# A graph layer's kernel: seven products of quarters for two product pairs in matrices 8 and 9 too

## The chip, the cores and the metric

The kernel runs on one core of one Trainium2 chip. Its time is the device time of one execution in microseconds (us); the time before is the median of three runs, 1374.24 us (1372.67 to 1378.07). A core has engines that run side by side, each through a queue of its own in order: TensorE (PE) multiplies, VectorE (DVE) and ScalarE (ACT) add, scale and copy, GpSimd (POOL) here mainly issues gathers and scatters by index, and SyncE (SP) issues plain transfers. ScalarE issues some transfers too. They meet through semaphores.

## The reference

One relational graph layer over 1250 nodes of 1024 features, 20000 edges and 8 edge types, with a highway gate; all in 32-bit floats:

```
h = max(layernorm(x), 0)
u = h @ root + bias
for r in 0..7:
    sums = segment_sum(h[src] where edge type is r, dst); cnt = count of such edges per dst
    u += (sums / max(cnt, 1)) @ weight[r]
z = concat(u, h) @ w_gate + b_gate
out = x + tanh(u) * z + h * (1 - z)
```

## The kernel before

Averaging over edges and multiplying by a weight can change places, so the kernel first multiplies h by every matrix and then gathers rows of the products by edge. The matrices are numbered s = 0 to 10: eight relation weights (0 to 7), root (8, `ROOT`), the lower half of w_gate, which multiplies h (9), and the upper half, which multiplies u (10). `NM` is 11, `R0` is (0, 3, 6, 8): the relations form three groups. Products of relations go to `y` in HBM, that of root to `hr_dram`, that of matrix 9 to `z_dram`; the last two get a bias added in `put` (L499), from the tile `bias_bc`.

**Steps.** The 1250 rows are ten blocks of up to 128 rows. `step(s, i)` multiplies two of them, blocks i and i + 5, by matrix s; `NP` = 5 steps make a matrix. Each is a 256x1024 by 1024x1024 product, done by the Strassen-Winograd scheme on halves: seven products (A11 B11, A12 B21, S1 T1, S2 T2, S3 T3, S4 B22, A22 T4) in `product`, each four matmuls of 128x512 (L377, which the trace records as two passes each). S1 to S4 are sums of quarters of h, kept in `h_op`; T1 to T4 are sums of quarters of the matrix, kept in nine buffers `wbuf` and made by VectorE (`make_t1` to `make_t4`, L169 to L181) around the end of the matrix before. Matrix 8's root and 9's and 10's weights are loaded from the last two steps of the matrix before on, by ScalarE's and SP's queues.

**Products of two neighbouring steps.** Two neighbouring steps use the same right operand, so their two 128-row products of one kind form a 256x512 by 512x512 product, and this can be done by the same scheme once more, on quarters: seven products of two 128x256 matmuls each (L214) in place of two of four 128x512 matmuls. Three classes do so:

- `Second`, for A12 B21 of steps 0 and 1, and of steps 2 and 3, in all matrices from 1 on.
- `Third`, for S4 B22 of the same two pairs, where `thirds(s)` holds: matrices 4 to 7.
- `Fourth`, for A22 T4 of steps 1 and 2, and of steps 3 and 4, in the same matrices.

`Third` and `Fourth` need sums of their quarters, made by VectorE just in time: `sums` (L270 to L273: s1, t1, s2, t2), and later `next_sums` (L276 to L279), which write the next values over them. They stand in the four tiles `room`, from a pool `inner` that is open while matrices 4 to 7 run. `first` makes three quarter products and has ScalarE copy two of them into a `part` tile (L294, L297); `last` makes three more, and `second` the seventh. VectorE adds them to the rows in `first_to` (L305, L306), `fifth_to` (L309) and `last_to` (L312 to L314, L329 to L333).

**Rows.** The results of a step are two row tiles of 128x1024 out of four `row` buffers. `put` stores a row with SP's queue when all of its parts have been added. With `Third` the first row of an even step is put in the step after it (from `then`), and with `Fourth` the second row of an odd step is put at the end of the step after it.

**Gathers.** Beside the products run the edges' sums, one group of relations beside two matrices: group 0 beside 4 and 5, group 1 beside 6 and 7, group 2 (`LG`) beside 8 and 9. For each block of nodes VectorE multiplies each gathered row by its weight and adds it to `u` (`add_slot`, L1218); GpSimd issues the gathers (L1210) into four `got` buffers. There are four `u` buffers. Beside 8 and 9 the blocks are taken in the order 4 to 9, 0 to 3, with 4, 4, 3, 3, 2, 2, 16, 7, 6 and 5 slots; a block's u is loaded by GpSimd (`rows_of`, L630), and the first six are stored by SP (`last_dram`, L1422) when done. Between matrices 7 and 8 stands a conditional branch for nodes with unusually many edges (L1353); it isn't taken in the traced execution.

The program is scheduled by hand: on each engine the instructions stand in the order in which the Python code issues them. `beside(j)` in `step` is called after each product of a step with j counting up, and decides what VectorE and the transfer queues get between products; gathers are spread evenly over these calls, at its end (`between`).

Of the kernel before, what the change touches and what calls it, by code (L numbers as in the profile page):

```python
# [9 lines left out]
F32 = mybir.dt.float32  # L10
# [9 lines left out]
def tile_rgcn_highway(  # L20
# [31 lines left out]
    nc = tc.nc  # L52
# [3 lines left out]
    P = 128  # L56
    N, D = x.shape
# [5 lines left out]
    H = Q // 2  # L63
# [4 lines left out]
    G = 3  # L68
    R0 = (0, 3, 6, R)
# [20 lines left out]
    def nrows(d):  # L90
        return min(P, N - d * P)
# [4 lines left out]
    def nedges(c):  # L96
        return P if c < NCH - 1 else EL
# [366 lines left out]
    ROOT = R  # L464
# [8 lines left out]

    def thirds(s):

        return R0[1] < s < ROOT

    def fourths(s, i):

        return (i - 1) // 2 * 2 + 1 if thirds(s) and i else None  # L480
# [3 lines left out]
    def step(s, i, between=lambda j: None, second=None):  # L484

        two = paired(s, i)
        t = [rows.tile([P, D], F32, name="row") for _ in range(2)]
# [5 lines left out]
        def put(i, part, t):  # L493
            d = i + part * NP
            n = nrows(d)
            at = slice(d * P, d * P + n)
            if s >= ROOT:
                to = (hr_dram, z_dram)[s - ROOT][at, :]
                nc.vector.tensor_add(t, t, bias_bc)  # L499
            else:  # L500
                g = max(k for k in range(G) if R0[k] <= s)
                o = (s - R0[g]) * N + d * P
                to = y[g][o:o + n, :]
            nc.sync.dma_start(to, t[:n])

        def beside(j):
# [17 lines left out]
            if q4 and i % 2 == 0 and j == 6:  # L524
                q4.last_to(to4, t[1][:, :Q])
                put(i - 1, 1, t4)
# [38 lines left out]
        if two:  # L565
            e, to = waiting[i - i % 2]
            if thirds(s):
                if i % 2 == 0:
                    waiting_third[i] = Third(fac[s], i, room)
                q = waiting_third[i - i % 2]  # L570
                q.holds = i % 2 == 0

                def then(c):
                    if q.holds:
                        q.second(c)
                    else:
                        q.last(c)
                        q.last_to(to[:, Q:], t[0][:, Q:], c)
                        put(i - 1, 0, to)

                q.then = then
            if i == 0:
                fill = dict(sixth=lambda: (e.second(), e.second_to_first(to)))
            elif i == 1:
                fill = dict(first=lambda: (e.first(), q and q.first(), 0)[-1],
                            fifth=lambda: (e.sixth(), True),
                            sixth=lambda: (e.seventh(), e.to_first(to), 0)[-1],
                            seventh=lambda: (e.fourth(), e.to_second(t[0]),
                                             q or put(i - 1, 0, to), 0)[-1],
                            third=lambda: (e.fourth_to_second(t[0]), 0)[-1])  # L590
            elif i == 2:
                fill = dict(sixth=lambda: (e.first(), q4 and q4.first(), q4)[-1],
                            seventh=lambda: e.sixth(),
                            third=lambda: (e.seventh(), e.to_first(to), 0)[-1],
                            fourth=lambda: (e.fourth(), not q4)[-1])
            else:
                fill = dict(first=lambda: (e.to_second(t[0]), e.fourth_to_second(t[0]), 0)[-1],
                            sixth=lambda: (e.second(), q and q.first(), True)[-1],
                            seventh=lambda: (e.second_to_first(to), q or put(i - 1, 0, to),
                                             0)[-1])  # L600
# [17 lines left out]
    idx = const.tile([P, G, ND, WIDE], I32, name="idx")  # L618
    rcp = idx.bitcast(F32)[:, :, :, SLOTS:]
    w_of = const.tile([P, G, ND, SLOTS], F32, name="w_of")  # L620
# [65 lines left out]
    with ExitStack() as early:  # L686
# [108 lines left out]
        for name, of, pad in (("dst", dst, G * KEYS), ("typ", etype, R), ("src", src, 0)):  # L795
            t = ix0.tile([P, 2, P], I32, name=f"e_{name}")
# [374 lines left out]
        while going[0]:  # L1171
            s, i = next(steps)
# [11 lines left out]
    with ExitStack() as edges_part:  # L1184
# [6 lines left out]
        room = [inner_pool.tile([P, 2, n], F32, name=f"inner{k}")  # L1191
                for k, n in enumerate((H, H, P, P))]
# [37 lines left out]
        def edges(g, blocks, to, late=0):  # L1230

            of = u_dram[g - 1] if g else None
            nb = len(blocks)
            starts = [late + sum(K[g][d] for d in blocks[:b]) for b in range(nb + 1)]
            leaves = [starts[b + 1] - 1 + GOT for b in range(nb)]
            reads = [max(-1, starts[b] - 5, leaves[b - UB] if b >= UB else -1) for b in range(nb)]
            u, then = {}, {}  # L1240
            for t in range(-1, leaves[-1] + 4):
                for b, d in enumerate(blocks):
                    if starts[b] <= t < starts[b + 1]:
                        k = t - starts[b]
                        add_slot(u[d], g, d, k, idx[:, g], w_of[:, g], first=g == 0 and k == 0)
                for b, d in enumerate(blocks):
                    if t == leaves[b]:
                        then[t + 3] = to(d, u[d])
                if then.get(t):
                    then[t]()  # L1250
                for b, d in enumerate(blocks):
                    if t == reads[b]:
                        u[d] = new_u(d, of, g)
                yield

        def u_back(g):
            def to(d, u):
                n = nrows(d)
                to_rows(u_dram[g][:, :], u[:n], node[:n, g, d:d + 1], f"u{g}")

            return to
# [42 lines left out]
        def beside(e, total, s, i, last):  # L1304


            between = spread(e, total, 7 * ((last - s) * NP + NP - i))
            while s <= last:
                step(s, i, between)
                s, i = next(steps, (NM, 0))  # L1310
            return s, i

        s, i = next(steps)
        while s <= R0[1]:
            step(s, i)
            s, i = next(steps)
# [8 lines left out]
        def with_others(e):  # L1325

            others = other_groups()
            for k, _ in enumerate(e):
                yield
                if k % 2:  # L1330
                    next(others, None)
            for _ in others:
                pass

        weights(0)
        s, i = beside(with_others(edges(0, range(ND), u_back(0))), sum(K[0]) + 2, s, i,
                      R0[2] - 1)
# [6 lines left out]
        for g in range(1, G - 1):  # L1344
# [3 lines left out]
            s, i = beside(e, sum(K[g]) + LATE + 1, s, i, R0[g + 2] - 1)  # L1348
# [4 lines left out]
        with tc.If(passes > 0):  # L1353
# [34 lines left out]
            with tc.For_i(0, passes, 1):  # L1388
# [9 lines left out]
                for c in range(NCH):  # L1398
                    n = nedges(c)
# [11 lines left out]


        inner_part.close()
        bias_bc = edges_part.enter_context(tc.tile_pool(name="bpool", bufs=1)).tile(
            [P, D], F32, name="bias_bc")
        nc.sync.dma_start(bias_bc, bias[None, :].to_broadcast([P, D]))
        LG = G - 1
        HELD = 4

# [59 lines left out]
        def gate_u(i, j):  # L1479

            if j == 2:
                for part, d, n in pair(i):
                    hs[part] = got()
                    rows_of(hs[part][:n], h_dram[:, :], node[:n, LG, d:d + 1])
                    nc.scalar.activation(place_of("d", i, part)[:n], us[d][:n], AF.Tanh)
            elif j == 3:
                for part, d, n in pair(i):
                    transposed(h_op[i % 2], part, us.pop(d), n)
                left(h_op[i % 2])
            elif j == 4:  # L1490
                for part, d, n in pair(i):
                    dt = place_of("d", i, part)
                    nc.vector.tensor_sub(dt[:n], dt[:n], hs[part][:n])
# [16 lines left out]
        while s < NM - 1:  # L1510
            def beside_h(j):
                between(j)
                if (s, i, j) == (ROOT + 1, 0, 0):
                    nc.sync.dma_start(bias_bc, b_gate[None, :].to_broadcast([P, D]))
                if (s, i) == (NM - 2, NP - 1):
                    gate_u(0, j)

            step(s, i, beside_h)
            s, i = next(steps, (NM, 0))

        for i in range(NP):
            t = [rows.tile([P, D], F32, name="row") for _ in range(2)]
# [54 lines left out]
            else:  # L1577
# [3 lines left out]
                                                                  bufs=2)))  # L1581
# [22 lines left out]
```

## Time and profile before

The profile is of one execution. Its engines' busy times by matrix are shown with the prediction; here is the frame.

| | |
|---|---|
| time of the profiled execution | 1378.07 us |
| its span (first to last instruction) | 1376.3 us |
| median of three runs | 1374.24 us |
| instructions | 13466 |
| granted TensorE clock, mean | 0.993 |
| start of matrices 4, 5, 6, 7 | 515.85, 636.57, 767.05, 882.63 |
| start of matrices 8, 9, 10 | 1003.41, 1122.17, 1240.93 |
| VectorE busy in matrices 8 and 9 | 68.48 and 76.18 us |
| matmul rows of 128x512 (L377), 128x256 (L214) | 2480 in `ps`; 288 and 248 in the two largest groups |

Times inside an execution are us from the span's start. A timeline line gives start, duration, engine, source line, operation, out<-in, and in brackets the idle time of the engine before it with what ended it. A matmul's shown duration overlaps the next one's, so the distance between starts is the true cost. "q" after an engine's name is its sequencer: it issues a transfer. A wait that is put down to an engine is the one that ended last.

### The profile page before, as it was taken

What the parts mean: (1) busy time and instruction counts of PE and PEld (TensorE: products, weight loads), DVE (VectorE), ACT (ScalarE), POOL (GpSimd) and SP (SyncE); (2) the same over time, 40 slices, a digit from 0 to 9 for tenths busy, and PEclk for the clock granted to TensorE, in tenths of its full rate; (3) what the DMA queues carried; (4) which work ended last, traced back from release to release, by engine and by line L of the source; (5) the groups of instructions that cost most, each with busy time, mean ns of one, the idle gap of its engine ahead of it and who ended that gap; (6) DMA issues with size and microseconds to landing.
All of it is one profiled execution on the core that took longest, in us unless ns stands there. A gap on an engine that the chain in (4) does not pass through costs nothing.

```text
span 1376.3 us, 13466 instructions
## 1 busy us (share of the span) xinstructions
PE 1343.0 (98%) x4002; PEld 698.1 (51%) x4002; DVE 1023.6 (74%) x2049; ACT 376.7 (27%) x824; POOL 653.7 (47%) x571
## 2 busy tenths in 40 slices
PE   9999999999999999998899999999999999999998
PEld 5444455455445545654465566556455445544443
DVE  7855967887884976877688778978765485567985
ACT  3335566565641111110111121111111111121220
POOL 0001655564562468647665344566534244435641
PEclk9999999999999999999899999999999999999999
DMA  8745566754763257288878647878866664586861
GB/s 318 265 181 144 94 127 150 197 92 109 174 164 112 57 163 171 70 298 168 257 229 319 201 141 259 300 254 296 318 208 241 219 251 137 179 300 216 279 222 58
DMA packets 110654, 273.06 MB, mean 198 GB/s; under 512 B 26020, under 2 KB 28434, under 8 KB 110448
## 3 DMA queue, kind: packets, MB, share of 16 engines
q0 software_dynamic: 48912, 128.60, 30.3%
q1 hardware_dynamic: 45536, 111.58, 27.2%
q10 hardware_dynamic: 16128, 31.98, 7.2%
q8 instruction: 32, 0.52, 0.2%
q14 instruction: 46, 0.38, 0.1%
HBM read 214.20 MB, written 80.89 MB: 214 GB/s over the span
## 4 chain that ended last, share of the span: by engine, by line
PE 57%; issue 15%; DMA 11%; DVE 9%; POOL 6%; ACT 1%; POOLq 0%; DVEq 0%; another core or an unknown queue 0%; ACTq 0%
PE ps L377 47%; DMA got<-y,idx 8%; PE ps L214 6%; DVE u L1218 2%; POOL got L1210 2%; DMA y<-row 2%; PE ps_q L214 1%; POOL node_dram L667 1%; POOL idx L630 1%; PE ps_n L377 1%; DMA node_dram<-ids,pos_i 1%; POOL got L630 1%; PE ps_n L947 1%; DMA got<-hr_dram,node 1%; POOL out_dram L636 1%
## 5 line engine op out<-in xcount | busy, mean ns | idle before, releaser
L377 PE MATMUL ps<-w,h_op 128*128 128x512 f32 x2480 | 1092.0, 594 | 15.6 <-ACT row L427 13.4
L377 PEld LDWEIGHTS ps<-w,h_op 128*128 128x128 f32 x2480 | 466.8, 190 | 551.8 <-issue 526.4
L1210 POOL DMA_INDIRECT got<-y,idx x202 | 266.5, 1319 | 241.3 <-DVE u L1218 173.6
L1218 DVE SCALAR_TENSOR_TENSOR u<-got,w_of,u 128x1024 f32<-128x1024 f32 (+1 forms) x192 | 245.9, 1282 | 113.7 <-DMA got<-y,idx 104.1
L1026 POOL DMA_INDIRECT table<-row_col,at_i x157 | 177.0, 1127 | 163.5 <-DVE at_i L1022 73.8
L402 DVE TENSOR_TENSOR row<-row,part 128x512 f32<-128x512 f32 x55 | 37.9, 689 | 70.6 <-ACT part L401 61.8
L453 ACT COPY row<-ps 128x512 f32<-128x512 f32 x50 | 29.2, 584 | 200.5 <-PE ps L377 127.2
L401 ACT COPY part<-ps 128x512 f32<-128x512 f32 x55 | 32.2, 585 | 174.7 <-PE ps L377 162.3
L416 ACT COPY row<-ps 128x512 f32<-128x512 f32 x55 | 32.2, 585 | 164.8 <-PE ps L377 144.5
L214 PE MATMUL ps<-w,w 128*128 128x256 f32 x288 | 71.3, 380 | 0.0
L427 ACT COPY row<-ps 128x512 f32<-128x512 f32 x55 | 32.2, 585 | 129.0 <-PE ps L377 120.7
L423 ACT COPY row<-ps 128x512 f32<-128x512 f32 x47 | 27.5, 585 | 138.8 <-PE ps L377 102.4
L667 POOL DMA_INDIRECT node_dram<-ids,pos_i x30 | 43.7, 1457 | 44.6 <-issue 44.3
L214 PE MATMUL ps<-w,h_op 128*128 128x256 f32 x248 | 64.2, 381 | 0.0
L214 PEld LDWEIGHTS ps<-w,w 128*128 128x128 f32 x288 | 54.4, 190 | 19.2 <-issue 13.2
L214 PEld LDWEIGHTS ps<-w,h_op 128*128 128x128 f32 x248 | 46.6, 190 | 24.7 <-issue 20.7
L952 DVE TENSOR_TENSOR seen<-seen,ps_n 128x110 f32<-128x110 f32 x157 | 42.2, 269 | 21.7 <-PE ps_n L947 10.0
L1012 DVE SCALAR_TENSOR_TENSOR junk<-k_bc,key_col,before 128x128 f32<-128x128 int32 x157 | 54.9, 350 | 4.2
L394 DVE TENSOR_TENSOR row<-row,ps 128x512 f32<-128x512 f32 x38 | 26.0, 685 | 42.2 <-PE ps L377 28.7
L929 ACT ACTIVATE is_lo<-io,less_lo 128x128 bf16<-128x128 f32 x157 | 50.1, 391 | 0.7 <-DMA xh_dram<-xt 0.7
L1080 DVE SCALAR_TENSOR_TENSOR junk<-v_bc,val,one 128x1280 bf16<-128x1280 f32 x30 | 46.5, 1550 | 0.8
L630 POOL DMA_INDIRECT u<-u_dram,node x20 | 20.4, 1020 | 51.3 <-DMA last_dram<-u 32.0
(223 smaller groups left out, 1328.5 us busy)
## 6 DMA issues: line engine op xcount, KB each, us to landing
y<-row SPq DMA_DIRECT2D x72, 512.0 KB
w<-in_L_gnn_weight_dram ACTq DMA_DIRECT2D x21, 1024.0 KB
w<-in_L_gnn_weight_dram SPq DMA_DIRECT2D x10, 1024.0 KB
k_bc<-keys_dram SPq DMA_DIRECT2D x39, 256.0 KB
l_bc<-los_dram SPq DMA_DIRECT2D x39, 256.0 KB
w<-in_L_gnn_w_gate_dram ACTq DMA_DIRECT2D x6, 1024.0 KB
h_dram<-h_op SPq DMA_DIRECT2D x9, 512.0 KB
hr_dram<-row SPq DMA_DIRECT2D x9, 512.0 KB
```

Of the source, the lines that this page charges most:

```text
L214: nc.tensor.matmul(p, a[:, k, :], b[:, k, :], start=(fresh and k == 0), stop=(k == 1), skip_group_check=True)
L377: nc.tensor.matmul(b[:, at], aop[:, i, k, :], w.of[i][:, k, at], start=(fresh and k == 0), stop=(k == KQ - 1), skip_group_check=True)
L402: nc.vector.tensor_add(c22, c22, d)
L630: nc.gpsimd.indirect_dma_start(out=to, out_offset=None, in_=of, in_offset=bass.IndirectOffsetOnAxis(ap=at, axis=0))
L667: ins = nc.gpsimd.indirect_dma_start(out=node_dram[g][:, :], out_offset=bass.IndirectOffsetOnAxis(ap=pos_i[:, g, d:d + 1], axis=0), in_=id ...
L929: nc.scalar.activation(is_lo[:, i, :], io, AF.Abs, bias=less_lo[:, c0 + i:c0 + i + 1])
L952: nc.vector.tensor_add(seen[j][:, i, :], was, p[:, i, :])
L1012: nc.vector.scalar_tensor_tensor(junk, o["k_bc"][:, i, :], key_col[:, c:c + 1], before, op0=OP.is_equal, op1=OP.mult, accum_out=rank[:, c: ...
L1026: ins = nc.gpsimd.indirect_dma_start(out=table[:, :], out_offset=bass.IndirectOffsetOnAxis(ap=at_i[:n, i:i + 1], axis=0), in_=row_col[:n, ...
L1080: nc.vector.scalar_tensor_tensor(junk, v_bc[:, g, :], val[:, c:c + 1], one.to_broadcast([P, KEYS]), op0=OP.is_gt, op1=OP.mult, accum_out=p ...
L1210: nc.gpsimd.indirect_dma_start(out=t[:n], out_offset=None, in_=y[g][:, :], in_offset=bass.IndirectOffsetOnAxis(ap=at[:n, d, k:k + 1], axis=0),
L1218: nc.vector.scalar_tensor_tensor(u[:n], t[:n], w, u[:n], op0=OP.mult, op1=OP.add)
```

## The change

`thirds` holds for every matrix after 3 up to 9 (matrix 10 is not made by `step`), so `Third` and `Fourth` are used in matrices 8 and 9. Their sums need a place when the pool `inner` has been closed: the two of 128x512 get tiles of a new pool, and the two of 128x256 are put over the part of the index tile `idx` that groups 0 and 1 no longer need. To make room, `bias_bc` becomes two pieces: 768 columns in a tile, and 256 columns over the part of `w_of` that belongs to groups 0 and 1. So a bias is loaded by two transfers and added by two instructions.

```diff
     def thirds(s):
 
-        return R0[1] < s < ROOT
+        return R0[1] < s
...
             if s >= ROOT:
                 to = (hr_dram, z_dram)[s - ROOT][at, :]
-                nc.vector.tensor_add(t, t, bias_bc)
+                for c, of in bias_bc:
+                    nc.vector.tensor_add(t[:, c], t[:, c], of)
...
         inner_part.close()
-        bias_bc = edges_part.enter_context(tc.tile_pool(name="bpool", bufs=1)).tile(
-            [P, D], F32, name="bias_bc")
-        nc.sync.dma_start(bias_bc, bias[None, :].to_broadcast([P, D]))
+
+
+        bpool = edges_part.enter_context(tc.tile_pool(name="bpool", bufs=1))
+        sums_at = idx[:, :G - 1].bitcast(F32).rearrange("p g d k -> p (g d k)")
+        room = [bpool.tile([P, 2, H], F32, name=f"sum{k}") for k in range(2)]
+        room += [sums_at[:, k * H:(k + 1) * H].rearrange("p (k n) -> p k n", k=2)
+                 for k in range(2)]
+        bias_bc = [(slice(0, D - H), bpool.tile([P, D - H], F32, name="bias_bc")),
+                   (slice(D - H, D),
+                    w_of[:, :G - 1].rearrange("p g d k -> p (g d k)")[:, :H])]
+
+        def load_bias(of):
+            for c, to in bias_bc:
+                nc.sync.dma_start(to, of[None, c].to_broadcast([P, c.stop - c.start]))
+
+        load_bias(bias)
...
                 if (s, i, j) == (ROOT + 1, 0, 0):
-                    nc.sync.dma_start(bias_bc, b_gate[None, :].to_broadcast([P, D]))
+                    load_bias(b_gate)
```

On VectorE the changed order puts, in matrices 8 and 9, the four instructions of `sums` and of `next_sums` between the gathers' additions: those of `Third` at the second call of `beside` in step 0 and the last in step 2 (`sums`), and in steps 1 and 3 (`next_sums`); those of `Fourth` at the end of steps 1 and 3, and in steps 2 and 4. On SP two stores of rows change places with stores of `last_dram`. GpSimd's order is as before.

## The prediction

> **What bounds the kernel now.** I read the page's busy shares first, then the busy times by matrix, then TensorE's timeline with its waits, last VectorE's timeline where the change puts new work. Columns of the second block: engine busy in that stretch, then TensorE's clock, DMA share, GB/s; its stretches run from the start of one matrix to the next, matrices 4 to 9.
>
> ```profile
> PE 1343.0 (98%) x4002; PEld 698.1 (51%) x4002; DVE 1023.6 (74%) x2049; ACT 376.7 (27%) x824; POOL 653.7 (47%) x571
> ```
> ```profile
> 515.85:636.57 120.72, 117.47 (x354) 67.54 (x353) 87.64 (x131) 20.59 (x41) 81.97 (x70) 0.99 0.64 180
> 636.57:767.05 130.48, 117.81 (x354) 67.26 (x353) 101.37 (x138) 20.29 (x41) 78.47 (x70) 0.96 0.82 246
> 767.05:882.63 115.58, 115.58 (x356) 66.55 (x355) 96.61 (x161) 20.58 (x41) 56.11 (x47) 1.00 0.66 229
> 882.63:1003.41 120.78, 117.66 (x353) 67.32 (x352) 99.19 (x130) 20.30 (x41) 66.61 (x59) 0.99 0.80 277
> 1003.41:1122.17 118.76, 118.76 (x305) 57.51 (x304) 68.48 (x79) 17.61 (x33) 44.16 (x36) 1.00 0.72 248
> 1122.17:1240.93 118.76, 118.76 (x317) 58.45 (x316) 76.18 (x84) 22.06 (x38) 47.52 (x33) 1.00 0.57 193
> ```
>
> TensorE sets the time. Matrices 8 and 9 are the simple case: 118.76 us each, no idle time at all. Matrices 4 to 7 already have what the change gives to 8 and 9, and they are the best evidence there is: one of them takes 115.58 us, but the others 120.72, 130.48 and 120.78, because TensorE waits in them. These are the products and those waits:
>
> ```profile
> 923.32 1.03 PE L214 MATMUL ps_q<-inner,inner 128*128 128x256 f32 x4
> 924.19 1.03 PE L214 MATMUL ps_n<-w,inner 128*128 128x256 f32 x4
> 926.78 3.60 PE L377 MATMUL ps<-w,h_op 128*128 128x512 f32 x8
> 930.21 3.60 PE L377 MATMUL ps_n<-w,h_op 128*128 128x512 f32 x8
> ```
> ```profile
> 605.75 2.05 PE L214 MATMUL ps_q<-inner,inner 128*128 128x256 f32 x4 [2.77 <-DVE inner L277]
> 660.08 5.34 PE L377 MATMUL ps<-w,h_op 128*128 128x512 f32 x8 [12.15 <-ACT row L427]
> 984.62 2.08 PE L214 MATMUL ps_q<-inner,inner 128*128 128x256 f32 x4 [2.90 <-ACT part L294]
> ```
>
> Start to start, a quarter product takes 0.865 us and a full one 3.43. The waits have two kinds: a sum that VectorE had not made yet (L277), and a copy by ScalarE that stood behind the copy into a row whose last store had not landed (at 660 and 984).
>
> **What it removes.** Two full products, 6.87 us, become seven quarter products, 6.05: 0.82 us less. Four such pairs in a matrix, two matrices: 8 x 0.82 = 6.5 us. The row of matrix 6 against that of matrix 8 says the same: 118.76 - 115.58 = 3.2 a matrix. TensorE had no idle time there, so this is all on the path, and 6.5 us is the most that can come back.
>
> **What it adds beside TensorE.** VectorE, per Third: eight sums (0.42 and 0.68 us by turns, 3.8 with the overlap of 0.08 between neighbours), 1.1 for the first addition, 0.4 for the fifth, 2.05 for the last, less two additions of 0.68 that go: 6.0. Per Fourth 3.8 + 1.1 + 1.5 = 6.4. Two of each: 25 us a matrix. Each of ten bias additions, 1.22 now, becomes one of 768 columns (0.95, between the rows of 512 and 1024) and one of 256 (0.42): 0.07 more. So VectorE goes from 68 and 76 to about 94 and 102 us of some 116, as busy as in matrices 4 to 7. ScalarE gains eight copies of 0.37 a matrix, hidden in its 100 idle us. GpSimd's order is unchanged. SP gets one more bias load (0.3 us to issue) twice; both lie where it waits. The sums' new place in the index tile makes the first sum of matrix 8 wait for the eight software DMA queues. GpSimd passes the same wait before it issues at 1016.1; VectorE comes to that sum at about 1018 (in the trace the operations ahead of it ended at 1019.5, with the first addition to a row among them), and TensorE wants it at 1028.3: 0, and no more than 0 unless those queues drain 10 us later.
>
> **What it moves: a sum behind a late gather.** This decides. VectorE takes its queue in order. In step 3 of matrix 8 it stands so:
>
> ```profile
> 1081.65 0.41 DVE L252 TENSOR_TENSOR row<-row,ps 128x256 f32<-128x256 f32 x1
> 1094.22 1.28 DVE L1218 SCALAR_TENSOR_TENSOR u<-got,w_of,u 128x1024 f32<-128x1024 f32 x1 [12.15 <-DMA got<-y,idx]
> 1095.74 1.29 DVE L1218 SCALAR_TENSOR_TENSOR u<-got,w_of,u 98x1024 f32<-98x1024 f32 x1 [0.24 <-DMA got<-y,idx]
> ```
> ```profile
> 1078.26 0.32 SPq L504 DMA_DIRECT2D hr_dram<-row  x1
> 1078.63 0.42 SPq L1422 DMA_DIRECT2D last_dram<-u  x1
> ```
> ```profile
> 1082.84 0.94 POOL L630 DMA_INDIRECT u<-u_dram,node  x1 [15.46 <-DMA last_dram<-u]
> 1084.09 0.99 POOL L1210 DMA_INDIRECT got<-y,idx  x1 [0.30 <-issue]
> ```
>
> VectorE waits 12.15 us for one gather, and today nobody minds. The chain: the store of a finished sum (last_dram) stands on SP behind the store of a row; GpSimd cannot load the next sum's start until that store has landed; the gather is issued behind it and lands ten us later, beside two 1 MB weight loads. The changed order puts next_sums (L276 to L279) directly behind this very addition, and the last three quarter products of step 3 need them.
>
> When does TensorE want them? From the matrix' start: step 0 has five full and two quarter products, 18.9 us; steps 1 and 2 four full and thirteen quarter ones, 25.0 each; in step 3 four full and four quarter products come first, 17.2. Together 86.0 us. The gather's wait ended at 1094.22 - 1003.41 = 90.8, and its addition and two sums take 2.4: 93.2, so 7.2 us late. The near end: today step 3 starts at 73.1 (21.5 + 25.8 + 25.8), then at 68.8; if the chain of stores comes 4.3 earlier too, 2.9 are left. The far end: the row store ahead of last_dram stands behind 1.3 us of bias and the sums of four pairs, and each earlier last_dram also sits behind a later row store, which holds up gathers 11 and 13 in turn. Adding the rows in queue order I come to that row store at about 78 instead of 74.9: 10.4 late. I take 7, the row as it stands. After 2.90 us of idle time the trace shows four half-passes in 1.87 us instead of 0.86, and two more 0.6 too long: 1.6 more. So 8.6.
>
> **The other waits.** Step 4: its second row was released by the store at the end of step 3, and ScalarE's copy of the first quarter product stands behind the copy into that row. In matrices 4 to 7 TensorE lost 0, 0.5, 0 and 4.5 there (2.90 + 1.6), mean 1.3; in 8 and 9 that store goes out 1.3 later, behind its bias additions. I take 2.5 each, 5; ends 0 and 11.6. Step 3 of matrix 9: the addition ahead of its sums ran at 1200.81 without a wait: 0 to 2.8 as at 605.75, I take 0.5. Start of matrices 9 and 10: three stores now wait for the last additions and 1.3 us of bias apiece; between 0 (as at 767 and 882) and the 12.15 at 660, I take 1.5 for both, nearest to the three quiet starts. Sum of waits 15.6, less 6.5: 9 slower.
>
> [...] The trace's granted clock is 0.72 of full speed between 984 and 990, after 2.90 us of idle time. [...]
>
> Gather issues on GpSimd take 984 ns at the least, and the one at 1124.91 took 5672 while VectorE made sums of two SBUF tiles and bias additions throughout. [...]
>
> **Rivals.** *The gain holds* (not slower): the gather of step 3 lands by 83.6 us after the matrix' start, 7.2 earlier than now, say because its last_dram goes out as soon as the sum is done (1060.8 by the rows). For it: matrix 6 lost 0.5 in all. Against: SP's order keeps last_dram behind the row store. Then 1374.2 - 6.5 + 1 to 3, about 1370.
> *Gain and waits cancel*: the near end, 2.9 + 1.6, and 4 elsewhere, or matrices like 4 and 7, which lost about 5 each: 1374.2 - 6.5 + 8.5 to 10.5, about 1377.
> *A long wait at a matrix' start*: VectorE, at 100 us of 116, reaches the last additions of step 4 as late as it did at 648, and the next matrix' copies stand still as at 660: 12 more on the forecast, 1395.
> *It does not do what it says*: were index and weight tiles treated as whole, gathers and sums would chain. GpSimd's order is the same and its gathers got no longer list of waits, so I give it no case of its own.
>
> **How the numbers follow.** The profiled execution took 1378.07 us (span 1376.3, 1.8 around it), 3.8 above the median of the three runs, 1374.24; differences are carried to the median: 1374.2 + 9 = 1383. Forecast 0.50 (own range 1379 to 1390), cancel 0.25 (1373 to 1379), gain holds 0.13 (1367 to 1372), long wait 0.12 (1390 to 1402). About 0.5%, 6.9 us, is what a measurement of this kernel tells from no change. Faster by that would need all of 6.5 and more: 0.03. Same: the rest of the gain, the cancelling case and the part of the forecast under 1381: 0.47. Slower: 0.50. The range 1369 to 1394 leaves out half of the two outer cases, about 0.1.
>
> **What would show it.** Right: a wait of TensorE of 3 to 10 us before ps_q<-sum,idx in step 3 of matrix 8 (about 1090), released by a sum on L277, with VectorE idle for a gather just before; 7 x 0.865 for every replaced pair; VectorE near 94 and 102. Wrong: matrices 8 and 9 at 115.5 without a wait, or the loss at a matrix' start behind a row's store.

## The result and the profile after

The changed kernel takes 1390.47 us (median of 5 runs, 1386.91 to 1391.72), the kernel before it on the same chip 1373.87 (5 runs, 1372.67 to 1378.07): a ratio of 1.0113, 95% interval 1.0091 to 1.0134, or 16.6 us slower. 1383 was predicted, with a range of 1369 to 1394. The profiled execution took 1389.10 us (span 1387.3, granted clock 0.986).

The busy shares of the changed kernel:

```profile
PE 1343.1 (97%) x4098; PEld 719.8 (52%) x4098; DVE 1071.5 (77%) x2169; ACT 382.7 (28%) x840; POOL 658.3 (47%) x571
```

TensorE is as busy as before (1343.1 us against 1343.0), although it has some 6 us of products less: part of them ran at a lower clock (0.96 in matrix 8 and in matrix 10, 1.00 in matrix 9, below). VectorE has 47.9 us more. Where the time went is seen by matrix: first two stretches of the kernel before (matrix 9 up to the first product of matrix 10, and matrix 10 up to the last product), then three of the changed kernel (matrices 8, 9 and 10). Columns: stretch, its length, busy time of PE, PEld, DVE, ACT and POOL, granted clock, DMA share, GB/s.

```profile
1122.17:1242.68 120.51, 120.51 (x321) 59.21 (x320) 77.93 (x85) 22.06 (x38) 47.52 (x33) 1.00 0.56 190
1242.68:1360.26 117.58, 116.86 (x322) 55.11 (x320) 97.16 (x115) 23.98 (x36) 59.07 (x53) 1.00 0.64 217
```
```profile
999.32:1124.74 125.42, 118.73 (x353) 68.65 (x352) 89.29 (x132) 20.45 (x41) 46.02 (x36) 0.96 0.67 231
1124.74:1242.33 117.59, 117.49 (x370) 68.30 (x369) 96.27 (x139) 24.98 (x46) 43.33 (x34) 1.00 0.57 190
1242.33:1371.26 128.93, 118.91 (x321) 55.70 (x320) 105.43 (x128) 23.92 (x36) 57.98 (x53) 0.96 0.61 206
```

(The start of matrix 10 at 1240.93 that stands ahead of the prediction and in it is 1.75 us early: it leaves out the transposes of u (L342) inside the last step of matrix 9, which so takes 120.51 us and not 118.76. All stretches from here on are counted to the first product of matrix 10.) Matrix 8 lost 6.7 us (118.76 to 125.42), matrix 9 gained 2.9, matrix 10, whose products were not touched, lost 11.4. Together 15.1. TensorE's timeline has one wait in each of the two that lost:

```profile
1082.17 3.60 PE L377 MATMUL ps<-w,h_op 128*128 128x512 f32 x8
1092.46 2.04 PE L214 MATMUL ps_q<-sum,idx 128*128 128x256 f32 x4 [6.69 <-DVE sum L277]
1094.30 1.91 PE L214 MATMUL ps_n<-w,idx 128*128 128x256 f32 x4
1096.01 1.91 PE L214 MATMUL ps<-sum,h_op 128*128 128x256 f32 x4
1097.71 1.41 PE L214 MATMUL ps<-w,h_op 128*128 128x256 f32 x4
```
```profile
1242.33 10.46 PE L377 MATMUL ps<-w,h_op 128*128 128x512 f32 x24
1262.09 5.50 PE L377 MATMUL ps<-w,h_op 128*128 128x512 f32 x8 [9.30 <-ACT row L423]
```

**Matrix 8.** 6.69 us of wait for a sum of `next_sums`, and then four quarter products that take 6.5 us from start to start instead of 3.46: 9.7, less a gain of 3.1. VectorE's timeline shows what the sum stood behind:

```profile
1077.32 0.41 DVE L252 TENSOR_TENSOR row<-row,ps 128x256 f32<-128x256 f32 x1
1090.09 1.28 DVE L1219 SCALAR_TENSOR_TENSOR u<-got,w_of,u 128x1024 f32<-128x1024 f32 x1 [12.36 <-DMA got<-y,idx]
1091.30 0.42 DVE L276 TENSOR_TENSOR idx<-h_op,h_op 128x256 f32<-128x256 f32 x1
1091.63 0.68 DVE L277 TENSOR_TENSOR sum<-w 128x512 f32<-128x512 f32 x1
```

The gather itself was issued by GpSimd behind the load of the next sum's start, which waited for the store of a finished sum to land:

```profile
1082.29 0.95 POOL L631 DMA_INDIRECT u<-u_dram,node  x1 [16.86 <-DMA last_dram<-u]
1083.55 0.99 POOL L1211 DMA_INDIRECT got<-y,idx  x1 [0.30 <-issue]
```

**Matrix 10.** ScalarE's copy into a row (L423) waits for a row's store, TensorE (the 9.30 us above) for this copy. Three rows are still to be stored when matrix 10 begins, with four row buffers in all (VectorE, then SP, then ScalarE):

```profile
1239.14 1.28 DVE L1219 SCALAR_TENSOR_TENSOR u<-got,w_of,u 128x1024 f32<-128x1024 f32 x1 [6.82 <-DMA got<-y,idx]
1250.07 2.29 DVE L177 TENSOR_TENSOR w<-w,w 128x2048 f32<-128x2048 f32 x1
1253.40 0.68 DVE L329 TENSOR_TENSOR row<-row,ps_q 128x512 f32<-128x512 f32 x1
1254.66 0.95 DVE L500 TENSOR_TENSOR row<-row,bias_bc 128x768 f32<-128x768 f32 x1
```
```profile
1255.98 3.91 SPq L505 DMA_DIRECT2D z_dram<-row  x3
```
```profile
1261.45 0.59 ACT L423 COPY row<-ps 128x512 f32<-128x512 f32 x1 [14.90 <-DMA z_dram<-row]
```

The last additions of `Fourth` to the second row of step 3 (L329) come at 1253.40, 11 us after TensorE had made what they add. VectorE reaches them only after a gather's addition that had waited 6.82 us, copies and sums of the next left operand, T2 and T3.

Three open rows do not cost anything by themselves. At the starts of matrices 6, 7 and 8 of the kernel before, and of matrix 9 of the changed kernel, three rows are left too, and TensorE does not wait. There the first of the three stores is issued 3.7 to 5.4 us after the matrix' first product; at matrix 10 it is 13.7, and at matrix 5 of the kernel before, with its 12.15 us of wait, 12.8. This is SP at the start of matrix 9 (1124.74) of the changed kernel:

```profile
1130.17 2.77 SPq L505 DMA_DIRECT2D hr_dram<-row  x3
```

So it takes both: three rows of four still open, and VectorE late with them.

### The profile page after: what moved, and what is told of

It reads as the page before. It is cut to its first block, busy times and chain, and to the rows that moved or that the text cites. A ratio compares the mean times of both kernels' runs of the same rounds, so it can differ in the third digit from the quotient of the medians.

```text
span 1387.3 us, 13837 instructions
## 1 busy us (share of the span) xinstructions
PE 1343.1 (97%) x4098; PEld 719.8 (52%) x4098; DVE 1071.5 (77%) x2169; ACT 382.7 (28%) x840; POOL 658.3 (47%) x571
## 4 chain that ended last, share of the span: by engine, by line
PE 59%; issue 14%; DVE 10%; DMA 9%; POOL 6%; ACT 1%; another core or an unknown queue 0%; SPq 0%; POOLq 0%; DVEq 0%; ACTq 0%
PE ps L377 44%; PE ps L214 7%; DMA got<-y,idx 6%; PE ps_q L214 3%; DVE u L1219 2%; PE ps_n L377 2%; POOL got L1211 2%; POOL node_dram L668 2%; DMA y<-row 1%; POOL idx L631 1%; PE ps_n L214 1%; DMA w<-in_L_gnn_weight_dram 1%; DMA node_dram<-ids,pos_i 1%; DVE h_op L358 1%; PE ps_n L948 1%
## 5 line engine op out<-in xcount | busy, mean ns | idle before, releaser
L377 PE MATMUL ps<-w,h_op 128*128 128x512 f32 x2320 | 1028.2, 595 | 21.6 <-ACT row L427 10.4
L377 PEld LDWEIGHTS ps<-w,h_op 128*128 128x128 f32 x2320 | 437.3, 191 | 520.3 <-issue 486.0
L1211 POOL DMA_INDIRECT got<-y,idx x202 | 271.5, 1344 | 237.6 <-DVE u L1219 189.6
L214 PE MATMUL ps<-w,h_op 128*128 128x256 f32 x264 | 68.7, 383 | 0.0
L427 ACT COPY row<-ps 128x512 f32<-128x512 f32 x55 | 32.3, 586 | 120.4 <-PE ps L377 111.7
L423 ACT COPY row<-ps 128x512 f32<-128x512 f32 x43 | 25.2, 586 | 139.3 <-PE ps L377 76.8
L214 PEld LDWEIGHTS ps<-w,h_op 128*128 128x128 f32 x264 | 50.1, 192 | 24.5 <-issue 19.2
L394 DVE TENSOR_TENSOR row<-row,ps 128x512 f32<-128x512 f32 x30 | 20.5, 684 | 32.1 <-PE ps L377 25.4
```

What stands on the lines that cost most here:

```text
L214: nc.tensor.matmul(p, a[:, k, :], b[:, k, :], start=(fresh and k == 0), stop=(k == 1), skip_group_check=True)
L377: nc.tensor.matmul(b[:, at], aop[:, i, k, :], w.of[i][:, k, at], start=(fresh and k == 0), stop=(k == KQ - 1), skip_group_check=True)
L1211: nc.gpsimd.indirect_dma_start(out=t[:n], out_offset=None, in_=y[g][:, :], in_offset=bass.IndirectOffsetOnAxis(ap=at[:n, d, k:k + 1], axis=0),
```

## The experiments

Runs of unchanged code differ by more than 10 us (the kernel before: 1367 to 1385 over all its runs here), and the profiles place this in the waits of matrices 4 to 7 (at the start of matrix 5, 12.15 us in the kernel before and 8.26 in the changed kernel, which is the same there). From the first product of matrix 8 on, profiles of kernels that are alike there repeat within 0.1 us where nothing waits. So the table gives, beside each ratio, the length of matrices 8, 9 and 10 in the profile, counted as above, and their sum against the 356.85 of the kernel before. A dash: not counted one by one.

| run | ratio to the kernel before (95%) | 8 | 9 | 10 | sum against before |
|---|---|---|---|---|---|
| changed kernel | 1.0113 (1.0091 to 1.0134) | 125.42 | 117.59 | 128.93 | +15.1 |
| m8_only | 1.0063 (1.0040 to 1.0086) | 124.71 | 120.50 | 117.58 | +5.9 |
| m9_only | 1.0048 (1.0031 to 1.0066) | 118.77 | 117.53 | 127.35 | +6.8 |
| store_by_gpsimd | 1.0095 (1.0078 to 1.0112) | 119.49 | 117.59 | 129.53 | +9.8 |
| sums_first | 1.0162 (1.0132 to 1.0192) | 130.08 | 117.59 | 129.26 | +20.1 |
| sums_before_addition | 1.0087 (1.0058 to 1.0117) | 124.39 | 117.58 | 129.52 | +14.6 |
| no_last_fourth_in_9 | 1.0053 (1.0017 to 1.0090) | 124.92 | 118.08 | 119.56 | +5.7 |
| t3_behind_row | 1.0086 (1.0053 to 1.0120) | 125.89 | 117.58 | 127.26 | +13.9 |
| early_pairs_only | 1.0006 (0.9987 to 1.0025) | 118.00 | 118.03 | 121.61 | +0.8 |
| places_only | 1.0001 (0.9978 to 1.0023) | - | - | - | 0.0 |
| matrices_4_and_7 | 0.9938 (0.9918 to 0.9957) | - | - | - | 0.0 |
| matrices_4_7_8 | 0.9915 (0.9888 to 0.9941) | - | - | - | -1.6 |

The theory ("order") is that two things stand late in a queue: in step 3 of matrix 8 sums behind an addition that waits for a gather, and at the end of matrix 9 the last additions to a row whose buffer matrix 10 needs. The main rival ("load") is that 25 us of added VectorE work a matrix must cost such waits somewhere, wherever it stands.

### Each matrix alone

```diff
-        return R0[1] < s
+        return R0[1] < s <= ROOT          # m8_only
+        return R0[1] < s and s != ROOT    # m9_only
```

> The change in matrix 8 alone; matrix 9 is done as before. Theory 'order': the loss of matrix 8 is one wait, 6.7 us before the second product of the last three quarter products of step 3 (around 1090), with a slow clock behind it, and the loss at the start of matrix 10 comes from the end of matrix 9 alone. So matrix 8 stays at about 125 us, matrix 9 is 118.8 without idle time, matrix 10 starts without a wait: 1374 + 6.7 = 1380 to 1381. Rival 'load' (25 us of added VectorE work a matrix make waits wherever the queue is tight): half of the added work gives about half of the loss spread over both matrices, and some wait stays at a start of matrix: 1380 to 1384 as well, so it is the trace that tells: where the waits are.

> The change in matrix 9 alone; matrix 8 is done as before. Theory 'order': matrix 8 takes 118.8 without idle time, matrix 9 takes 117.6 at most (or 115.6, its full gain of 3.2), and the wait of about 9 us at the start of matrix 10 is there, with about 2 us of slow clock behind it: 1374 - 3 + 11 = 1382. Rival 'carried over' (the wait at the start of matrix 10 is the end of a delay that began in matrix 8 and was passed on through stores and gathers): with matrix 8 as before it is gone or under 3 us, and the time is 1371 to 1374.

Each wait stays with its matrix. With matrix 8 alone TensorE waits in step 3 and nowhere after; with matrix 9 alone, at the start of matrix 10 and nowhere else from matrix 8 on. The line of each, m8_only first:

```profile
1089.12 2.04 PE L214 MATMUL ps_q<-sum,idx 128*128 128x256 f32 x4 [6.37 <-DVE sum L277]
```
```profile
1248.57 5.28 PE L377 MATMUL ps<-w,h_op 128*128 128x512 f32 x8 [7.92 <-ACT row L423]
```

Little is carried over: the rival of m9_only asked for under 3 us at the start of matrix 10 and got 7.92. It is 9.30 to 9.82 in the four runs that have the change in both matrices with the end of matrix 9 as it is, so some 1.5 us of it seem to come from matrix 8. The two losses, 5.9 and 6.8, add to 12.7 of the 15.1. The gain is there in each: 117.53 us for matrix 9 where it was 120.51, and for matrix 8 115.7 without its wait and the slow clock (124.71 less 6.37 and 2.6).

### Matrix 8: what the sums stand behind

```diff
         def to_last(d, u):
-            nc.sync.dma_start(last_dram[d * P:d * P + n, :], u[:n])
+            nc.gpsimd.dma_start(last_dram[d * P:d * P + n, :], u[:n])   # store_by_gpsimd
```

> The changed kernel, with the store of a block's finished sums issued by GpSimd's queue in place of SP's. It takes away SP's order (this store behind the store of a row); VectorE's work, its order and its load stay. Theory 'order': in step 3 of matrix 8 the gather is issued several us earlier, the sums behind its addition are made in time, and the wait of 6.7 us and the slow clock behind it go, about 9.8 us; the start of matrix 10 has another cause and keeps its 9 us: 1390.5 - 9.8 = about 1381. Rival 'load': VectorE has as much to do as before, so TensorE waits as long, there or somewhat later: 1388 to 1393.

VectorE waits 4.20 us for the gather instead of 12.36, and the wait for the sum is gone. In its place stand two shorter ones, both for a copy by ScalarE (L294) that follows a copy into a row not stored yet; matrix 10 keeps its own:

```profile
1086.89 1.13 PE L214 MATMUL ps_q<-sum,idx 128*128 128x256 f32 x4 [0.98 <-ACT part L294]
1105.96 1.13 PE L214 MATMUL ps_q<-sum,idx 128*128 128x256 f32 x4 [2.46 <-ACT part L294]
1260.63 6.05 PE L377 MATMUL ps<-w,h_op 128*128 128x512 f32 x8 [9.33 <-ACT row L423]
```

Matrix 8 takes 119.49: 5.9 of the 9.7 us came back, not 9.8 as the theory said, since 3.4 went to what is late next. By the medians the run is 13.4 above its kernel before (1382.77 against 1369.39), where the forecasts, set against 1374, meant 7 for the theory and 14 to 19 for the load: the number alone would speak for the load. The trace tells them apart: the theory's wait went, and a third of it came back at places that have a cause of their own.

The next run was to put the sums ahead of the waiting addition by putting calls of `between` in step 3 off:

```diff
-            between(j)
+            if (s, i) == (ROOT, 3) and j in (2, 3):   # sums_before_addition: 1, 2, 3 here and below
+                if j == 3:
+                    between(2)
+                    between(3)
+            else:
+                between(j)
```

> The changed kernel; in step 3 of matrix 8 alone the gathers of the third call between products are put off to the fourth, so that the next values of the sums stand ahead of the addition that waits for its gather, not behind it. Gathers, stores and VectorE's work are the same. Theory 'order': the wait of 6.7 us in step 3 goes; the gather's addition is as late as before, so step 4's rows and sums may be late in its place, by 0 to 5 us: 1381 to 1386. Rival 'load': the time stays at 1388 to 1393, since the same work is done in the same span.

This moved nothing: those two calls hold nothing that stands before the sums, and in matrices 8 to 10 the order on every engine came out as in the changed kernel. It tells nothing of the theory, but it is a repeat of the changed kernel on the chip of the three runs above: 22 us over its kernel before, with waits of 8.10 and 2.83 us in matrix 8 where the first profile had 6.69 alone. So a kernel with such waits repeats only within some 5 us, and against this repeat the store by GpSimd's queue is worth 8.7 us by the medians. With j from 1 on exactly one addition changes its place:

> The changed kernel with one addition of VectorE moved: in step 3 of matrix 8 the addition that waits for its gather stands behind the next values of the sums and the first additions to the row, not ahead of them (the earlier try at this left every engine's order as it was). Theory 'order' in its full form: the wait of 6.7 us ahead of the sums goes, but the gather lands as late as before, at about 1090, and VectorE still has some 11 us of work (two more additions of gathers, the last additions to the rows, the bias) between it and the store that step 4 needs; TensorE, now 9.8 us earlier, stands there instead. So a wait of 5 to 9 us in step 4, put down to a copy of ScalarE behind a row's store, and 0 to 4 us less than the changed kernel: 13 to 19 above the kernel before. A smaller form ('only the sums were late'): no new wait over 2.5 us, 9 us less than the changed kernel: 7 to 10 above the kernel before.

```profile
1095.72 1.10 PE L214 MATMUL ps_q<-w,h_op 128*128 128x256 f32 x4 [1.07 <-DVE row L314]
1098.96 1.13 PE L214 MATMUL ps<-sum,idx 128*128 128x256 f32 x4 [2.15 <-DVE sum L271]
1103.13 2.08 PE L214 MATMUL ps_q<-sum,idx 128*128 128x256 f32 x4 [3.03 <-ACT part L294]
```

The sum is now made at 1080.41, and the wait of step 3 is gone; 6.25 us of others are back in step 4, in three pieces and not in the one that was expected. Matrix 8 gains 1.0 (124.39), the whole kernel is 13.6 us over its kernel before by the medians. The gather lands as late as ever (VectorE waits until 1088.62, 90.8 us after the start of the matrix, as in the changed kernel), and all that VectorE does behind it, sums, additions to rows, bias and so the stores, is late by that. This is the better description: not one instruction in an unlucky place, but a late gather with a queue behind it. An earlier gather (store_by_gpsimd) was worth 5.9 us in the profile, a better place for one instruction 1.0; since repeats of this wait differ by up to 4.7 us (125.42 and 130.08 above), the 1.0 by itself is not clear of noise, and the waits that came back are what tells.

### Matrix 10: the third row

```diff
     def fourths(s, i):
-        return (i - 1) // 2 * 2 + 1 if thirds(s) and i else None
+        return (i - 1) // 2 * 2 + 1 if thirds(s) and 0 < i < (NP if s <= ROOT else 3) else None
```

> The changed kernel; in matrix 9 alone A22 T4 of steps 3 and 4 is done as two full products again, so that the second row of step 3 is finished and stored in step 3. Theory 'late row': the wait at the start of matrix 10 (9.3 us and 2 of slow clock) goes or falls under 2, matrix 9 gives back 0.8; the wait in step 3 of matrix 8 stays. So 9 to 11 us less than the changed kernel: 6 to 9 above the kernel before. Rival 'load': VectorE has only a quarter of its added work less in matrix 9, so a wait of 5 us or more stays there: 12 to 16 above the kernel before.

With A22 T4 of the last two steps as two full products the second row of step 3 is stored in step 3. At the end of matrix 9 two rows are left to store, and ScalarE's copy waits for the product only (SP, then ScalarE):

```profile
1248.09 1.57 SPq L505 DMA_DIRECT2D z_dram<-row  x2
```
```profile
1246.05 0.59 ACT L423 COPY row<-ps 128x512 f32<-128x512 f32 x1 [2.89 <-PE ps L377]
```

The wait at the start of matrix 10 is gone, and the sum over the three matrices is 9.4 us less. It is not quite quiet: in the second step of matrix 10 a new wait of 1.76 us stands, for an addition of VectorE (L1544). The median (1383.18 against 1373.80) says 7 us less than the changed kernel's 16.6; this run's times spread from 1376 to 1389. The theory had said 6 to 9 above the kernel before, the rival 12 to 16; it is 9.4.

```diff
-                elif j == 5:
+                elif j == 5 and s < NM - 2:
                     new.make_t3()
...
                 q4.last_to(to4, t[1][:, :Q])
                 put(i - 1, 1, t4)
+            if (s, i, j) == (NM - 2, NP - 1, 6):
+                new.make_t3()
```

> The changed kernel; at the end of matrix 9 alone make_t3 (2.29 us on VectorE) stands behind the last additions to the second row of step 3 and its bias, not ahead of them. Theory 'late row': the store goes out 2.3 us earlier and the wait at the start of matrix 10 falls from 9.3 to about 7.0; T3 is not needed before the same place. So 2 us less than the changed kernel, 13 to 18 above the kernel before. Rival (the row's store is not what is waited for, or T3 takes its place): the wait stays at 9 or more.

One instruction of 2.29 us ahead of the row's additions was moved behind them; the wait fell to 7.52 us, 1.78 less, and matrix 10 took 1.67 less:

```profile
1260.02 5.60 PE L377 MATMUL ps<-w,h_op 128*128 128x512 f32 x8 [7.52 <-ACT row L423]
```

The store went out 2.4 us earlier relative to the start of matrix 10, and 1.78 of it reached TensorE; in the four runs above, which leave this place alone, the wait differs by 0.5. So the store of that row is what TensorE waits for. VectorE does the same work in this run, so it speaks against the load as such.

### The places

```diff
-        return R0[1] < s
+        return R0[1] < s < ROOT
```

> The seven quarter products stay in matrices 4 to 7, as in the kernel before; only the places are those of the changed kernel: the bias in two pieces, the sums' tiles over the index tile set aside and not used. Every theory that puts the loss on waits behind the new sums and rows expects no change: within 2 us of the kernel before. Rival 'places' (the bias in two loads and two additions, or sharing a tile with indices and weights, costs waits of its own): 4 us or more above it.

The median is 0.1 us under that of its kernel before (the ratio of all runs is 1.0001), and matrices 8 to 10 take 356.84 us. The bias in two pieces and the shared tiles cost nothing that can be seen.

### A version that is faster than both

> A try at a version that keeps the gain: the store of a block's finished sums by GpSimd's queue, and A22 T4 of steps 3 and 4 as two full products in matrices 8 and 9, so that no row is left to be stored at the end of step 3. Theory: matrix 8 loses 0.8 of its 3.2 and keeps a wait of about 1 in step 3; matrix 9 loses 0.8 of its 2.9; the start of matrix 10 is quiet. So 1.4 + 2.1 = 3.5 us under the kernel before, ratio 0.9975; ends 0.993 and 1.002. Rival 'load': VectorE still has some 19 us of added work in each of the two matrices, so 3 us or more above the kernel before.

This is the edit of `fourths` above with `s < ROOT` for `s <= ROOT`, and the store by GpSimd's queue. It equals the kernel before and keeps nothing of the gain. Matrix 8 behaved (118.00: 0.8 less and a wait of 1.38), matrix 9 too (2.5 less than before), but matrix 10 lost 4.0 again, at a place that was not foreseen:

```profile
1287.55 0.93 PE L342 MATMUL ps<-ident,u 128*128 128x128 f32 x4 [2.12 <-DVE row L1544]
```

VectorE enters matrix 10 some 1.3 us later relative to TensorE than before, the first addition there that has to wait for a gathered row of `hr_dram` comes 3.0 us later, and in the second step TensorE waits for VectorE's additions (L1544). Of the 4.0, 2.12 are this wait and 1.7 the clock after it. That this comes from matrix 9's faster end fits two other runs: no_last_fourth_in_9, with the same matrix 9, has it too (1.76 us), and matrices_4_7_8, which leaves matrix 9 as it was, does not. It was not tried by itself.

The wait of 12.15 us at the start of matrix 5, which the kernel before has, stands before the same copies (L423, L427), behind three stores of rows. So the same edit was made there, in the kernel before:

```diff
-        return (i - 1) // 2 * 2 + 1 if thirds(s) and i else None
+        return (i - 1) // 2 * 2 + 1 if thirds(s) and 0 < i < (3 if s in (R0[1] + 1, ROOT - 1) else NP) else None
```

> The kernel before, with one edit of the same kind as the one that made the start of matrix 10 quiet: A22 T4 of steps 3 and 4 as two full products in matrices 4 and 7. Theory 'late row': at the end of matrix 4 three rows are still to be stored where there are four buffers, and the next matrix' first products wait 8 to 14 us for them (around 657) in every profile so far; with the second row of step 3 stored in step 3 only two are left, and this wait goes, with about 1.6 of slow clock; in matrix 7 the wait of 2 to 4.6 us in step 4 goes as well. Each costs 0.8. VectorE is late at the start of matrix 5 too, so part of it comes back as small waits. Forecast 12 us under the kernel before, ratio 0.991; ends 17 and 4 under. Rival 'load' (VectorE's work as such): TensorE waits as long elsewhere in matrix 5, within 3 us of the kernel before.

Two stores instead of three at the end of matrix 4, as SP's timeline has it for the kernel before and for this one, and then this one's busy shares and its longest wait:

```profile
649.40 1.52 SPq L504 DMA_DIRECT2D y<-row  x3
```
```profile
641.36 0.78 SPq L504 DMA_DIRECT2D y<-row  x2
```
```profile
PE 1344.3 (99%) x3978; PEld 693.2 (51%) x3978; DVE 1011.6 (74%) x2023; ACT 375.6 (28%) x820; POOL 652.3 (48%) x571
```
```profile
686.68 5.24 PE L377 MATMUL ps_n<-w,h_op 128*128 128x512 f32 x8 [4.59 <-DVE row L312]
```

Both waits are gone, at the start of matrix 5 and in step 4 of matrix 7. A part returns as a wait of 4.59 us inside matrix 5, for VectorE. The ratio is 0.9938 (10.4 us by the medians; 12 were forecast, and the rival allowed 3). The edit also takes 12 us of work from VectorE, so this run alone does not separate a late row from load. With matrix 8's early pairs as well:

> As the run for matrices 4 and 7, and in matrix 8 the changed kernel's seven quarter products for S4 B22 of both pairs and A22 T4 of steps 1 and 2, with the store of finished sums by GpSimd's queue; matrix 9 as before. Matrix 8 took 118.0 so, against 118.76: 0.8 less than the run for matrices 4 and 7, if matrix 10 stays quiet; the wait of 2.1 us in matrix 10 that came up in the run of early pairs belongs to matrix 9's faster end and should not be there. Ratio 0.990 to 0.991; ends: 2 us less and 3 us more than the run for matrices 4 and 7.

The ratio is 0.9915 (0.9888 to 0.9941), 12.4 us under its kernel before (1367.75 against 1380.16), and 1.6 us less in matrices 8 to 10. It is the fastest kernel of this study, and it does fewer of the replaced products than the changed kernel does. Its lead over matrices_4_and_7 is within the intervals, and in its profile matrix 7 has a wait for a copy behind a row's store again (3.73 us, in step 3). Both gains are under 1%.

## Why the prediction was right, and where it was not

The sign was right, and for the reason that carried it; the size came out 7.5 us short, mainly since one term was taken far too small.

- **The gain, 6.5 us.** Nearly right: 6.0, of which 3.1 in matrix 8 (125.42 less 9.7 of wait and clock is 115.7, against 118.76) and 2.9 in matrix 9.
- **The deciding term, sums behind a late gather: 7 + 1.6.** The wait measured 6.69. The prediction had TensorE asking 86.0 us after the matrix' start and the sums 93.2 after it; it asked at 86.4 and went on at 93.1. That the size fits so well is in part luck. The gather was ready 90.8 us after the start both times, but by two changes that cancel: GpSimd issued it 84.2 us after the start and not 80.7, 3.5 later (the store of the finished sum was issued 1.3 us later behind its row, and landed 2.2 us more slowly), which is on the way to the prediction's far end; and VectorE went on 6.5 us after that issue and not 10.1. With the later issue and the old 10.1 the wait would have been about 10 us, by an estimate from these rows. Why the gather landed faster was not tried. The clock was under-sized, 3.0 in place of 1.6: it was taken from one wait, and over all profiles this cost differs by as much (last section).
- **Step 4, 2.5 us each.** Measured: none. In matrix 8 TensorE came to step 4 late by the wait of step 3, and the store had landed by then. Take the first wait away and it is there: 2.46 in store_by_gpsimd. It was a wait in the shade of another, and the two should not have been added. Matrix 9 had no earlier wait to hide one, and none came in its step 4 either, nor the 0.5 us in its step 3.
- **Start of matrices 9 and 10, 1.5 for both.** This step failed. Matrix 9 lost nothing, matrix 10 lost 11.4. The prediction took the quiet starts of three matrices as nearest, and had the 12.15 us at 660 as the far end. Three rows are open in all four, so what sets the price is how late VectorE comes to them, and the trace had this to go by: before 660 VectorE had waited 5.66 and 3.25 us for gathers at the end of the matrix, and in the kernel before matrix 9 ends in such a wait too (2.38 us at 1233.96), with gate work and 1.3 us of bias on top. The third rival ("a long wait at a matrix' start") named the mechanism, with a chance of 0.12 and 12 us; it came in addition, at matrix 10.
- **VectorE, 94 and 102 us.** 89.29 and 96.27; the rest of the work slid behind the end of the matrix (105.43 in matrix 10 against 97.16). The total, 47.9 more, is near the 50 predicted.
- **The bias split and the shared places, 0.** Right: places_only; and in the changed kernel the first sum in the index tile passes its four semaphore instructions, 21 to 50 ns each, at 1015.0 to 1015.3, and runs at 1015.58 with no idle time of VectorE ahead of it.
- **GpSimd's issues.** The prediction names one gather issue of 5.67 us, beside sums of two SBUF tiles and bias additions on VectorE. Over matrices 8 and 9 the 52 gather issues averaged 1.40 us before and 1.31 in the changed kernel, with some 36 us more of such additions on VectorE; one of 5.28 is there too. The mean issue was no longer with the added work; what makes a single issue long stays open.

In sum: 15.6 us of waits less 6.5 were predicted; 21.1 less 6.0 were measured. The total came closer than its parts: step 4 was 5 us too high, the start of matrix 10 about 10 too low.

## What to carry to other kernels

Before a step is put into an in-order queue, look at what it will stand behind, and count what else stands behind that: if an operand lands late, bringing it earlier can be worth more than moving one instruction ahead of it (here 5.9 us against 1.0). Where results go out through a few buffers, count how many are still to be stored when the next stage begins, and how late the engine that finishes them comes to them; a scheme that keeps one more result open until the end of a stage can cost more than the products it saves (here 11.4 us in matrix 10 against 2.9 in matrix 9). And a wait already in the trace, at one place, prices the same arrangement at another better than quiet places do, where the work behind it is as late (12.15 us at matrix 5, 9.30 at matrix 10).

## What was not expected of the hardware

The clock after a wait. Over the thirteen profiles, TensorE's waits after the first 150 us sort so: of 30 of 0.9 to 2 us two were followed by a granted clock of 0.5; of 24 of 2 to 3 us 16 were and 8 were not; all 30 of 3 us or more were. What it cost, counted as the share of clock missing in the ten us after the wait, was 1.5 to 3.1 us, with no regard to the wait's length (1.5 after 8.10 us, 3.0 after 6.69). The three waits of sums_before_addition that stand within ten us of each other are left out of this range. Clock column (the third from the end) of the changed kernel around the wait of matrix 8, which begins at 1085.8:

```profile
1086.00:1088.00 2.00, 0.00 (x0) 0.00 (x0) 0.00 (x0) 0.45 (x1) 1.52 (x2) 1.00 0.88 289
1088.00:1090.00 2.00, 0.00 (x0) 0.00 (x0) 0.00 (x0) 0.00 (x0) 0.51 (x1) 0.56 0.80 219
1092.00:1094.00 2.00, 1.54 (x4) 1.30 (x5) 1.97 (x5) 0.00 (x0) 1.19 (x1) 0.50 0.10 20
1098.00:1100.00 2.00, 2.00 (x7) 1.33 (x7) 1.97 (x4) 0.59 (x1) 0.90 (x1) 0.88 0.81 270
```

Here the clock falls some 2.5 us into the wait, and comes back about 6 us after the work does. What sets the 16 waits of 2 to 3 us that were followed by the slow clock apart from the 8 that were not, these profiles do not show.
